# Layer 0 of a two-layer network: five attention stages of a slot queued one to two slots later

## The chip, the cores and the metric

The kernel runs on one core of a Trainium2 chip. The metric is device time in microseconds (us), the median over runs. A profile of one further execution shows what each engine did: TensorE (PE; PEld is its weight load), VectorE (DVE), ScalarE (ACT), GpSimd (POOL), and SyncE (SP), which here only issues DMAs.

## What is computed

The input is 8 images of 128x128 positions with 128 channels, in float32. Layer 0 is a linear attention with a normalization and a residual; layer 1 is a convolution, four selective scans and a gated normalization. The change touches layer 0 alone, whose reference is, cut to what matters:

```
qkv = einsum('bhwc,cf->bhwf', x, w_qkv)
q, k, v = split(qkv, 3)                     # each reshaped to (B, 4 heads, 32, N), N = H*W
q = softmax(q, axis=-2) * inv_scale         # over the 32 of a head
k = softmax(k, axis=-1)                     # over all positions
context = einsum('bhdn,bhen->bhde', k, v)
attn = einsum('bhde,bhdn->bhen', context, q)
out = einsum('bhwf,fc->bhwc', attn, w_out) + b_out
mu = mean(out); var = mean(square(out - mu))
out = (out - mu) * rsqrt(var + LN_EPS) * gamma + beta
return out + x
```

Layer 1 needs, beside this output, a gate z * sigmoid(z) of a projection of it; the kernel computes that gate within layer 0 too, by means of tanh.

## The kernel before

The program has three parts that run one after the other: `layer0`, `layer1_front` and `layer1_scan`. The profile is divided at about 2205 us, where the last gate of layer 0 is done.

In `layer0` an image of 128x128 positions is cut into 32 groups of 512 positions (`NG`), with the 128 channels on the partitions. Three kinds of work are staged over groups:

- **Context of an image** (`context(b)`): keys (`key`), a running maximum over blocks of four groups (`larger`, `fold`, `spread`), values (`value`), the difference to the maximum and its exponential (`subtract`, `raise_to`), and the sum of products k*v (`add`), which accumulates in PSUM and ends in a normalized 128x128 matrix.
- **Attention of an image** (`attend(b)`), which needs that matrix: `query` (PE pq; DVE qm, then q), `exponent` (ACT on q), `normalize` (DVE qs and its reciprocal, POOL's product with q), `through_wo` (PE pg, ACT copy gt), `through_context` (PE po, DVE o with the bias added, ACT square sq), `variance` (DVE var), `scale` (POOL: var, rstd by a power, and d, a diagonal of rstd), `turn` (PE pt, which scales and transposes), `finish` (ACT x1t, POOL's residual sum into x, and the store).
- **Gates of an image**: `ready` (a transposing copy v of a group, on POOL for the first gate of the coming slot and on ACT for the second, where the image's place asks for it), `gate_project` (two products pz on PE), `gate_tanh` (two on ACT), `gate_store` (two z on DVE, then two stores).

The order of the work is written out by hand. The loop of `image(b)` runs over slots `t`, and each slot calls every stage with the group that it treats: attention of image b for group t less a lag, and context of image b+1 for group a = t - `laters[b]`. The context manager `in_order` makes each engine keep exactly the order in which the stages were called. So an instruction that waits holds up everything behind it on its engine, and SP's stores keep that order as well.

Gates are planned beforehand (`plan`): while image b is attended, first the gates left over from image b-1 go out, two in a slot, then, once the attention of image b is through, its own gates, one in a slot. `laters[b]` is the number of slots needed for the left-over gates, plus two (`LEAD`), after which the context of the next image begins. The last image has no next context; its slots carry one left-over gate and, from slot 5 on, one of its own. So an image of the middle of the run consists of slots with attention and two gates, then slots with attention and a beginning context ("thin" slots), then slots with attention and context ("full"), and at the end slots with context and one own gate.

All small PSUM results of layer 0 (pq, pg, pz, pk, pv, po, pt and one of the maximum) share one pool of six buffers that go round: a new tile takes the buffer of the sixth before it, and waits until that has been read. SBUF buffers are q 3, gt 2, o 3, sq 2, d 2, z 4, v 4.

Of the kernel before, what the change touches and what calls it, by code (L numbers as in the profile page):

```python
# [26 lines left out]
NG = W // GW  # L27
# [50 lines left out]
def layer0(ctx: ExitStack, tc, xT, w_qkv, w_out, b_out, gamma, beta, win, x1, zs):  # L78
# [64 lines left out]
    def load(b, pieces=range(8)):  # L143
        for i in pieces:
            s = slice(16 * i, 16 * i + 16)
            nc.sync.dma_start(xs[b % 2][:, s, :], xT[ORDER[b], :, s, :])
# [3 lines left out]
    def ready(b, g, copy):  # L150

        v = group(b, g)
        if ORDER[b] % K < 2 or ORDER[b] < B // 2:
            t = wp.tile([P, GW, P], F32, name="v", bufs=4)
            copy(t, xs[b % 2].rearrange("p w h -> p h w")[:, g * GW : (g + 1) * GW, :])
            if ORDER[b] < B // 2:
                nc.sync.dma_start(x1[ORDER[b]][:, g * GN : g * GN + GN], t.rearrange("p w h -> p (w h)"))
            if ORDER[b] % K < 2:
                v = t
        vs[b, g] = v  # L160

    def gate_project(b, g):
        v = vs.pop((b, g))
        for c in range(NC2):
            pzs[b, g, c] = pz = ps.tile([P, GW, P], F32, name="pz", tag="ps")
            nc.tensor.matmul(pz, wz[:, c * P : c * P + P], v, start=True, stop=True)

    def gate_tanh(b, g, c):
        zts[b, g, c] = z = wp.tile([P, GW, P], F32, name="z", bufs=4)
        nc.scalar.activation(z, pzs[b, g, c], AF.Tanh)  # L170

    def gate_store(b, g, c):

        z = zts.pop((b, g, c))
        nc.vector.scalar_tensor_tensor(z, z, 1.0, pzs.pop((b, g, c)), ALU.add, ALU.mult)
        nc.sync.dma_start(zs[ORDER[b], c][:, g * GN : g * GN + GN], z.rearrange("p w h -> p (w h)"))
# [163 lines left out]
    for b in range(-1, B):  # L340
        left = NG - done[b - 1] if b > 0 else 0
        if b >= 0:
            laters[b] = -(-left // 2) + LEAD if left else 1
        for t in range(laters[b] + NG + BK + 2 if b < B - 1 else NG + 5):
            gates = plan[b, t] = []
            for _ in range(2 if b < B - 1 else 1):
                if b > 0 and done[b - 1] < NG:
                    gates.append((b - 1, done[b - 1]))
                    done[b - 1] += 1
                    if done[b - 1] == NG and b + 1 < B:  # L350
                        loads[b, t] = b + 1
            if b < B - 1:
                own = b >= 0 and not gates and t > NG + 2
            else:
                own = done[b] <= t - 5
            if own and done[b] < NG:
                gates.append((b, done[b]))
                done[b] += 1
# [4 lines left out]
    def image(b):  # L363

        key = larger = fold = spread = value = subtract = raise_to = add = None
        query = exponent = normalize = through_wo = through_context = None
        variance = scale = turn = finish = None
        if b + 1 < B:
            key, larger, fold, spread, value, subtract, raise_to, add = context(b + 1)
        if b >= 0:  # L370
            (query, exponent, normalize, through_wo, through_context, variance, scale, turn,
             finish) = attend(b)

        def at(stage, g):
            if stage is not None and 0 <= g < NG:
                stage(g)

        for t in (t for i, t in times if i == b):
            a = t - laters[b]
            first, second = (plan[b, t] + [None, None])[:2]  # L380
            at(scale, t - 2)
            at(finish, t - 3)
            at(query, t)
            at(through_wo, t - 1)
            for gates in plan[b, t]:
                gate_project(*gates)
            at(exponent, t)
            if first:
                for c in range(NC2):
                    gate_tanh(*first, c)  # L390
            at(subtract, a - BK - 1)
            at(raise_to, a - BK - 1)
            at(key, a)
            at(normalize, t)
            for gates, copy in zip(plan.get(then.get((b, t)), ()), (nc.gpsimd.tensor_copy, nc.scalar.copy)):
                ready(*gates, copy)
            if first:
                for c in range(NC2):
                    gate_store(*first, c)
            if second:  # L400
                for c in range(NC2):
                    gate_tanh(*second, c)
            at(fold, a - 1)
            at(value, a - BK - 1)
            at(larger, a)
            at(through_context, t - 1)
            if second:
                for c in range(NC2):
                    gate_store(*second, c)
            at(add, a - BK - 2)  # L410
            at(turn, t - 2)
            at(spread, a - 1)
            at(variance, t - 1)
            if (b, t) in loads:
                load(loads[b, t])

    with in_order(tc):
        load(0)
        load(1)
        for b in range(-1, B):  # L420
            image(b)
# [828 lines left out]
@with_exitstack  # L1250
def tile_kernel(ctx: ExitStack, tc, a, out):
    dram = ctx.enter_context(tc.tile_pool(name="dram", bufs=1, space=DRAM))
    x1 = dram.tile([B, P, L], F32, name="x1")
    ubs = dram.tile([B, 2, NC2, P, L], F32, name="ubs")
    xds = dram.tile([B, R + 2, L], F32, name="xds")
    xps = dram.tile([B, 2, 3, R + 2, L], BF16, name="xps")
    zs = dram.tile([B, NC2, P, L], F32, name="zs")
    gs = dram.tile([2, NC2, P, L], F32, name="gs")
    layer0(
        tc, a["x"], a["L0_conv_w_qkv"], a["L0_conv_w_out"], a["L0_conv_b_out"],  # L1260
        a["L0_conv_gamma"], a["L0_conv_beta"], a["L1_conv_Win"], x1, zs,
    )
    layer1_front(
        tc, x1, a["L1_conv_Win"], a["L1_conv_conv_w"], a["L1_conv_conv_b"], a["L1_conv_Wxproj"],
        a["L1_conv_D_param"], ubs, xds, xps, gs,
    )
    layer1_scan(
        tc, ubs, xps, zs, gs, a["L1_conv_dt_weight"], a["L1_conv_dt_bias"], a["L1_conv_A_log"],
        a["L1_conv_gamma"], a["L1_conv_beta"], a["L1_conv_Wout"], out,
    )  # L1270
# [40 lines left out]
```

## Time and profile before

| | us |
|---|---|
| median of 3 runs | 9080.09 (9077.24 to 9088.33) |
| profiled execution | 9087.79 |
| its span | 9086.0 |
| mean granted TensorE clock | 0.797 (1.00 in layer 0, 0.73 after it) |

| busy us | PE | PEld | DVE | ACT | POOL | DMA share |
|---|---|---|---|---|---|---|
| 0 to 2205 us (layer 0) | 2099.17 | 1283.15 | 1652.08 | 1370.79 | 1296.33 | 0.32 |
| 2205 to 9086 us (layer 1) | 4204.77 | 1805.48 | 6454.91 | 5663.61 | 6161.82 | 0.75 |

A row gives how long each engine was busy in that stretch. Matmuls are pipelined and their ends are modelled, so PE counts as busy for longer than its array is fed; the distance between the starts of successive matmuls is the better measure, and the one used below. Layer 0 is less than a quarter of the span, and layer 1 begins where it ends.

The largest waits within layer 0 (from 0 to 2080 us), with their sums and counts, are POOL's var for DVE's var (346.4 us, 237), ACT's sq for DVE's o (260.1 us, 195), POOL's q for DVE's qs (249.8 us, 21, one of them 115.9 us long before the first attention), ACT's exponential for DVE's q (170.2 us, 196) and DVE's var for ACT's sq (126.6 us, 176). PE waits 79.9 and 27.6 us for POOL's d, and 113.4 and 25.2 us for POOL's q (weight loads and matmuls).

### The profile page before, as it was taken

How to read it: one execution, taken by the hardware profiler on the slowest of the kernel's cores; microseconds unless marked ns; L12 is line 12 of the kernel's file. 1: busy time of each engine (PE TensorE's matmuls, PEld its weight loads, DVE VectorE, ACT ScalarE, POOL GpSimd, SP SyncE). 2: the span in 40 equal slices, each digit the busy share in tenths (PEclk: the TensorE clock that was granted, in tenths of full speed). 3: DMA queues.
4: the chain of work that ended last, by engine and by line, in shares of the span. 5: the costliest groups of instructions: out<-in, count | busy, mean ns of one | idle time of the engine just before them, and what ended most of it. 6: DMA issues, size and time to landing. Idle time of an engine off the chain costs nothing. (4 is left out here: it accounts for less than half of the span.)

```text
span 9086.0 us, 92120 instructions
## 1 busy us (share of the span) xinstructions
PE 6303.9 (69%) x24512; PEld 3088.6 (34%) x24512; DVE 8107.0 (89%) x8210; ACT 7034.4 (77%) x8046; POOL 7458.1 (82%) x4820
## 2 busy tenths in 40 slices
PE   8999999998999999997335436355373453634636
PEld 5556655564333333332003104022040230411403
DVE  6777777777999999998899999999999999999996
ACT  5666666665999999997788887888878788888785
POOL 3656766646789888887699998999989989999897
PEclk9999999999999999999557658566585575755757
DMA  1332323423687888889569578596785866858767
GB/s 77 140 119 110 130 98 149 164 94 135 217 245 255 249 242 243 244 243 258 157 176 258 168 213 235 167 259 179 206 244 159 242 197 193 255 153 231 217 177 209
DMA packets 934776, 1750.72 MB, mean 193 GB/s; under 512 B 150228, under 2 KB 376148, under 8 KB 926064
## 3 DMA queue, kind: packets, MB, share of 16 engines
q1 hardware_dynamic: 873328, 1509.92, 50.4%
q0 software_dynamic: 60928, 234.90, 14.0%
q8 instruction: 200, 3.28, 0.1%
q14 instruction: 320, 2.62, 0.1%
HBM read 1052.36 MB, written 692.12 MB: 192 GB/s over the span
## 5 line engine op out<-in xcount | busy, mean ns | idle before, releaser
L992 POOL TENSOR_TENSOR h<-ubt,sp 128x1024 f32<-128x1024 f32 x1024 | 2420.6, 2396 | 348.3 <-ACT mv L1099 112.4
L975 PE MATMUL px<-rows,dtw 128*128 128x512 bf16 x2048 | 953.5, 565 | 2263.8 <-DVE y L1042 1052.7
L575 DVE SCALAR_TENSOR_TENSOR acc<-xb,cw,acc 128x1024 f32<-128x1024 f32 x1024 | 1320.6, 1290 | 132.2 <-ACT xb L543 89.3
L567 POOL TENSOR_TENSOR tap<-tap 128x1024 f32<-128x1024 f32 x512 | 1223.1, 2392 | 248.8 <-ACT tap L565 224.9
L979 ACT ACTIVATE sp<-px 128x1024 f32<-128x1024 f32 x1024 | 1046.9, 1024 | 432.8 <-PE px L975 416.3
L975 PEld LDWEIGHTS <-dtw 128*128 128x128 bf16 x2048 | 169.0, 110 | 3087.5 <-issue 1022.8
L1002 DVE TENSOR_TENSOR_SCAN h<-px,h 128x1024 f32<-128x1024 f32 x512 | 1177.7, 2332 | 32.2 <-POOL h L992 29.1
L1000 DVE TENSOR_TENSOR_SCAN h<-px,h 128x1024 f32<-128x1024 f32 x512 | 1178.2, 2331 | 21.4 <-POOL h L992 18.7
L1050 POOL TENSOR_TENSOR y<-y,h 128x512 f32<-128x512 f32 x768 | 1162.8, 1561 | 3.9 <-DVE h L1023 3.9
L983 ACT ACTIVATE px<-sp,sa 128x1024 f32<-128x1024 f32 x1024 | 1110.4, 1109 | 6.1
L556 PE MATMUL acc<-xi,wt 128*128 128x512 f32 x2048 | 939.1, 601 | 54.1 <-ACT ures L580 54.1
L565 ACT ACTIVATE tap<-xb,cw 128x1024 f32<-128x1024 f32 x768 | 837.3, 1139 | 13.9 <-POOL xb L540 13.8
L979 ACT ACT_TABLE_LOAD x512 | 656.9, 1283 | 171.1 <-PE px L975 148.9
L983 ACT ACT_TABLE_LOAD x512 | 656.9, 1283 | 9.2
L1115 PEld LDWEIGHTS px<-wg,z 128*128 128x128 f32 x4096 | 582.8, 227 | 116.7 <-issue 110.8
L1115 PE MATMUL px<-wg,z 128*128 128x128 f32 x4096 | 581.9, 310 | 0.0
L1008 PE MATMUL pc<-rows,csel 128*128 128x512 bf16 x1024 | 517.6, 586 | 80.2 <-DVE rstd L1103 76.5
L556 PEld LDWEIGHTS acc<-xi,wt 128*128 128x128 f32 x2048 | 375.4, 190 | 575.5 <-issue 413.8
L286 POOL TENSOR_TENSOR q<-q,qs 128x512 f32<-128x512 f32 x256 | 270.3, 1056 | 313.8 <-DVE qs L285 249.8
L529 PE MATMUL pxb<-xi,wi 128*128 128x512 f32 x1024 | 498.2, 609 | 2.3 <-DMA xi<-x 1.2
L1042 DVE TENSOR_TENSOR y<-y,px 128x1024 f32<-128x1024 f32 x384 | 468.7, 1221 | 14.4
L1023 DVE TENSOR_TENSOR h<-h,pc 128x1024 f32<-128x1024 f32 x384 | 466.0, 1214 | 0.0
(154 smaller groups left out, 14923.0 us busy)
## 6 DMA issues: line engine op xcount, KB each, us to landing
ubt<-ubs SPq DMA_DIRECT2D x1024, 512.0 KB
zs<-z SPq DMA_DIRECT2D x512, 256.0 KB
ubs<-ures SPq DMA_DIRECT2D x256, 512.0 KB
ubs<-turned SPq DMA_DIRECT2D x256, 512.0 KB
z<-zs SPq DMA_DIRECT2D x256, 512.0 KB
y<-gs POOLq DMA_DIRECT2D x128, 1024.0 KB, 10.4
gs<-du POOLq DMA_DIRECT2D x96, 1024.0 KB, 8.7
rows<-xps SPq DMA_DIRECT2D x1536, 60.0 KB
```

Of the source, the lines that this page charges most:

```text
L556: nc.tensor.matmul(acc[:, s, :], wt[:, j, c, :], x, start=(j == 0), stop=(j == len(ON_PE) - 1))
L565: nc.scalar.activation(t, at(n, c, *d), AF.Copy, scale=weight(n, c, *d))
L567: nc.gpsimd.tensor_tensor(sums[n, c], sums[n, c], t, ALU.add)
L575: nc.vector.scalar_tensor_tensor(acc, at(n, c, *d), weight(n, c, *d), acc, ALU.mult, ALU.add)
L975: nc.tensor.matmul(p[:, hf * 512 : hf * 512 + 512], sl.dw[:, c * P : c * P + P], src, start=True, stop=True)
L979: nc.scalar.activation(t, da[n, c], AF.Softplus)
L983: nc.scalar.activation(da[n, c], sp[n, c], AF.Exp, scale=sa[:, sl.s, c : c + 1])
L992: nc.gpsimd.tensor_tensor(h, u, t, ALU.mult)
L1000: nc.vector.tensor_tensor_scan(e[:, ::-1], x[:, ::-1], e[:, ::-1], start, ALU.mult, ALU.add)
L1002: nc.vector.tensor_tensor_scan(e, x, e, start, ALU.mult, ALU.add)
L1050: nc.gpsimd.tensor_tensor(v[:, c], v[:, c], h[:, c], ALU.add)
L1115: nc.tensor.matmul(po[:, w, :], z[:, c, w * H : w * H + H], wg[:, c, :], start=(c == 0), stop=(c == NC2 - 1))
```

## The change

The stages themselves and their number stay the same. The lags and the order of their calls within a slot change:

- `normalize` treats group t-1 instead of t, and is called first in the slot.
- `through_context` treats t-2 instead of t-1, and is called ahead of the gates.
- `variance` treats t-3 instead of t-1, and is called ahead of `scale`.
- `scale` and `turn` treat t-3 instead of t-2, and `finish` t-4 instead of t-3.
- `through_wo` still treats t-1, but is called behind the gates' products, the first gate's tanh and the keys; `key` moves ahead of `raise_to`.
- The own gates of an image start one slot later, since the last group is finished one slot later. By the planner's rule the number of slots becomes 415 instead of 412, and `laters` changes from 16, 12, 11 and 11 to 17, 13, 12 and 12 for images 1, 3, 5 and 7.

```
-                own = b >= 0 and not gates and t > NG + 2
+                own = b >= 0 and not gates and t > NG + 3
...
-            at(scale, t - 2)
-            at(finish, t - 3)
+            at(normalize, t - 1)
+            at(variance, t - 3)
+            at(scale, t - 3)
+            at(finish, t - 4)
             at(query, t)
-            at(through_wo, t - 1)
+            at(exponent, t)
+            at(through_context, t - 2)
             for gates in plan[b, t]:
                 gate_project(*gates)
-            at(exponent, t)
             if first:
                 for c in range(NC2):
                     gate_tanh(*first, c)
             at(subtract, a - BK - 1)
+            at(key, a)
+            at(through_wo, t - 1)
             at(raise_to, a - BK - 1)
-            at(key, a)
-            at(normalize, t)
             for gates, copy in zip(plan.get(then.get((b, t)), ()), (nc.gpsimd.tensor_copy, nc.scalar.copy)):
                 ready(*gates, copy)
...
             at(fold, a - 1)
             at(value, a - BK - 1)
             at(larger, a)
-            at(through_context, t - 1)
             if second:
                 for c in range(NC2):
                     gate_store(*second, c)
             at(add, a - BK - 2)
-            at(turn, t - 2)
+            at(turn, t - 3)
             at(spread, a - 1)
-            at(variance, t - 1)
```

## Prediction

> **What bounds the kernel now.** I read the page first: its slices show where TensorE (PE) is full. Layer 0, all that the change touches, ends near 2205 us, so it is the first ten of 40 slices.
>
> ```profile
> PE   8999999998999999997335436355373453634636
> ```
>
> That reads as "PE-bound", but matmul busy time includes pipelining, so next I read PE's timeline at one full slot (attention and context work together, no gate).
>
> ```profile
> 1014.21 1.02 PE L272 MATMUL pq<-x,wq 128*128 128x512 f32 x2
> 1015.07 1.05 PE L292 MATMUL pg<-wo,q 128*128 128x128 f32 x8
> ...
> 1018.54 1.06 PE L244 MATMUL pc<-vt,k 128*128 128x129 f32 x8
> 1019.43 1.06 PE L325 MATMUL pt<-d,o 128*128 128x128 f32 x8
> 1020.32 1.02 PE L272 MATMUL pq<-x,wq 128*128 128x512 f32 x2
> ```
>
> Start to start, a product over 512 columns takes 0.86 us and a group of eight 0.89 us; the slot is 6.11 us with no gap. A gate pair is 4 passes, 1.72 us. So PE's work in a slot is: full 6.11; two gates 6.94 (0.86+0.89+3.44+0.86+0.89); one gate 5.22; attention alone 3.50, with the keys 4.36. Where is a slot longer? I took the starts of pq from the same view:
> - two gates: 6.94 in images 3 and 4, 7.0 to 7.8 in 1, 2, 5, 6. Nearly no loss.
> - full: 6.11. No loss.
> - the 9 thin slots between the last gate and the full ones: image 2 has 6.24, 5.05, 5.10, 5.05, 5.69, 5.64, 7.36, 5.22, 6.59 where PE's work is 3.50, 3.50, 4.36 (four times), 4.70, 5.22, 6.11.
> - image 7, one gate: 6.24 against 5.22.
>
> Starts less work, over layer 0, leave 163 us of PE stall: 11 before image 0, 18 in image 0, 107 in images 1 to 6, 28 in image 7. The 107 divide into 20 in two-gate phases, 73 in thin ones, 14 in the drains. What ends these waits is in VectorE's (DVE's) timeline, image 7:
>
> ```profile
> 2109.73 0.69 DVE L284 TENSOR_REDUCE qs<-q 128x16 f32<-128x512 f32 x1 [0.69 <-ACT q L279]
> 2110.45 0.25 DVE L285 RECIPROCAL qs<-qs 128x16 f32<-128x16 f32 x1
> 2110.62 1.22 DVE L175 SCALAR_TENSOR_TENSOR z<-z,pz 128x512 f32<-128x512 f32 x2
> 2111.75 0.68 DVE L300 TENSOR_TENSOR o<-po,bb 128x512 f32<-128x512 f32 x1
> 2113.19 0.69 DVE L306 TENSOR_REDUCE var<-sq 128x4 f32<-128x512 f32 x1 [0.76 <-ACT sq L302]
> 2113.80 0.68 DVE L274 TENSOR_REDUCE qm<-pq 128x16 f32<-128x512 f32 x1
> 2114.58 0.69 DVE L276 TENSOR_TENSOR q<-pq,qm 128x512 f32<-128x512 f32 x1
> 2115.97 0.69 DVE L284 TENSOR_REDUCE qs<-q 128x16 f32<-128x512 f32 x1 [0.69 <-ACT q L279]
> ```
>
> From qs to qs is 6.24 us, the slot itself. In-order queues close a ring: qs, reciprocal, two z, o, ScalarE's (ACT's) square, var, qm, q, ACT's exponential, qs. DVE leaves its queue's head to wait for ACT twice per slot. So the bound in thin and one-gate slots is this ring, not an engine. The same sum without the z is 5.1, with one more DVE operation 5.65: the thin slots' pitches. The method holds, and I use it on the new order.
>
> Two queues set the other limits. GpSimd (POOL) in a thin slot, and ACT in a two-gate slot:
>
> ```profile
> 699.29 1.04 POOL L286 TENSOR_TENSOR q<-q,qs 128x512 f32<-128x512 f32 x1
> 700.75 0.19 POOL L312 TENSOR_SCALAR var<-var 128x4 f32<-128x4 f32 x1 [0.41 <-DVE var L306]
> 701.02 1.02 POOL L314 TENSOR_TENSOR rstd<-var,half 128x4 f32<-128x4 f32 x1
> 702.12 1.04 POOL L317 TENSOR_TENSOR d<-ident,rstd 128x512 f32<-128x512 f32 x1
> 703.11 1.27 POOL L331 TENSOR_TENSOR x<-x1t,x 128x512 f32<-128x512 f32 x1
> 704.35 1.05 POOL L286 TENSOR_TENSOR q<-q,qs 128x512 f32<-128x512 f32 x1
> ```
>
> POOL's five instructions without their one wait (0.41) take 4.6 us: more than PE's 3.50 or 4.36.
>
> ```profile
> 659.20 0.63 ACT L279 ACTIVATE q<-q 128x512 f32<-128x512 f32 x1 [1.34 <-DVE q L276]
> 660.01 1.31 ACT L170 ACTIVATE z<-pz 128x512 f32<-128x512 f32 x2 [0.18 <-DMA zs<-z]
> 661.22 1.11 ACT L155 COPY v<-x 128x512 f32<-128x512 f32 x1
> 662.23 1.09 ACT L170 ACTIVATE z<-pz 128x512 f32<-128x512 f32 x2
> 663.19 0.64 ACT L302 ACTIVATE sq<-o 128x512 f32<-128x512 f32 x1
> ```
>
> The square stands last, behind both gates' tanh. This is what the change reverses.
>
> **What the Trainium skill says.** "Trainium Kernel Development and Optimization", Best Practices, advises against matmul busy time as a measure; the trace agrees (a one-gate slot looks 90% busy, 72.23 of 80 us in the table of stretches from 2110, with work of 5.22 in 6.24). "Perfetto Trace Analysis", DVE / Act Engine Instruction, puts the semaphore wait in a queue ahead of the engine and outside the profiled duration: hence starts, not durations, are added here. "ScalarE: Activation LUTs", What ACT_TABLE_LOAD costs, lets back-to-back activations overlap by about 93 ns; the trace shows 0.60 us tanhs 0.50 apart. "TensorE: Matmul & The Clock Gate", What's actually happening, gives half clock after an idle window; in image 7 the passes after a stall of 3 us take 0.85 instead of 0.43 us.
>
> **The change, part by part.** No instruction is added or removed. Each attention group runs one slot deeper, and the own gates of an image start one slot later, so 415 slots instead of 412; work per slot thins accordingly, and three more thin slots cost nothing that PE's work sum doesn't hold.
>
> *What goes.* The old ring is cut: exponential to qs and square to var now have most of a slot between them.
>
> *What comes, two-gate slots.* New DVE order: qs, reciprocal, var, qm, q, o, z a, z b, z c, z d. New ACT order: x1t, exponential, square, tanh a, b, gt, copy of v, tanh c, d. Behind the square, which waits for o, all four tanhs now stand; behind gt, which waits for PE's pg after the gate products, stand the copy and two tanhs. A new ring closes, from z c to the next z c, each step start to start in the two views above: z d 0.60, qs 0.60, reciprocal 0.73, var 0.17, qm 0.60, q 0.79, o 0.60, square 0.78, tanh a 0.52, tanh b 0.50, gt 0.50, copy 0.48, tanh c 0.97, z c 0.63: **8.45 us**, against 6.94 of PE. PE is drawn along, since a gate product takes the PSUM buffer that z c frees six tiles before. The old order's longest ring by the same sum is 6.5, below PE. POOL (4.6 and a copy of 1.0) fits. SP's queue too: copy's end to the next tanh over the z stores is 3.95 (663.55 to 667.50), with tanh b, gt and copy 6.6.
>
> Two-gate slots of images 1 to 6: 14, 6, 10, 8, 9, 9. Start: the first four slots are ramped; z c of slot 0 comes at 6.7 us as in image 3's trace (902.46 less 895.72), then 13.9, 21.8, 30.2, so the gate product of slot 4 starts at 31.0 where PE's work is 24.2: 6.8 lost. Each later slot loses 1.5; there are 26 of these. At the end pg waits for the last z d, qs, reciprocal and q's product: 3.1, and 0.8 more in five images with a single gate left. Sum 40.8+39.0+22.6 = 102, less the 20 stalled now: **+82**.
>
> *Thin slots.* Ring gone; now POOL's 4.6 binds, and DVE where it folds the maximum (two slots of about 5). The eight intervals after the first pg: 5.0+4x4.6+4.9+5.2+5.2 = 38.7 against work of 34.4, so 4.3 and 0.7 for the fold's wait: 5 an image, 30 instead of 73: **-43**.
>
> *Drains.* d is ready a slot ahead; the copy of v after the last group and the wait of pmx stay. About 1 of 2.3 an image: **-6**. *Image 0:* its first pg waits 3.6 instead of 4.5, and its seven thin slots go as above: **-7**.
>
> *Image 7.* No copies. Two gates: ring 7.5 (8.45-0.97) against 6.94 on 13 slots, +7. One gate: z a, z b 0.57, qs 0.56, reciprocal 0.72, var 0.17, qm 0.61, q 0.78, o 0.60, square 0.78, tanh 0.54, z 0.63 = 5.96 against 6.24 on 13 slots, -4. Start and tail lose about 2 less. **+1**, in which ±8 is open.
>
> *At nothing:* full slots (from 1010 to 1058 us DVE is busy 39.9, ACT 31.2, POOL 35.5 of 48; if that cover went, each 0.1 us costs 15 us over 150 slots), context-only slots with own gates, the next image's loads (landed well before the first keys: 11.6 us after issue now, some 9.4 then, while DMA moves 1 MB in about 2.5 us at the 420 GB/s of that stretch). Layer 1 runs the same code later or earlier; nothing hides layer 0.
>
> Sum: 82-43-6-7+1 = **+27 us** on the profiled 9087.8 (span 9086.0, 1.8 around it), so 9115. The median of the runs, 9080.1, is 7.7 less; carried over: **9107**.
>
> **Rivals.** *The new ring doesn't bind two-gate slots (faster).* Place: tanh behind square and gt. It decides at 6.94: if o and the square come early enough there, these phases lose 6 instead of 20 and image 7 gains 8 more: -14-43-6-7-7 = -77, **9003**. For it: from 640 to 676 us ACT is busy only 26.3 of 36. Against: low busy shares didn't prevent the 6.24 ring. Chance 0.14. *The ring binds, but half as hard* (7.7 us, by earlier starts): 30 us less, no change, **9077**. Chance 0.20. *Full slots lose too (slower still):* gt and the value copy, now late in PE's order, hold ACT 0.35 us a slot: +52, **9159**. Against: 1.5 us of room. Chance 0.10. That the order isn't what it says can't be: each engine keeps the order written.
>
> **How the numbers follow.** Main case 0.56, alone 9085 to 9130. A difference under 0.2% (18 us) can't be told from no change. Slower: 0.50 of the main case, 0.05 of the second rival and the third, 0.65; faster: the first and 0.04 of the second, 0.18; same: the rest, 0.17. Range 9045 to 9150, where thin slots gain 20 more and lose 20 less.
>
> **What would show it.** Right: two-gate slots of images 1 to 6 at 8.4 to 8.5, image 7's at 7.5 and 6.0, thin slots at 4.6 to 5, ACT's z waiting behind sq and gt, no wait of var for sq. Wrong: two-gate slots at 6.94, or full slots above 6.2.

## The result, and the profile after

| | before | after |
|---|---|---|
| median of 5 runs, us | 9083.94 (9077.24 to 9088.33) | 9121.03 (9115.49 to 9126.21) |
| ratio to before | | 1.0042, interval 1.0031 to 1.0053 |
| profiled execution, us | 9087.79 | 9121.03 |
| last gate product of layer 0 ends at | 2204.9 | 2249.1 |

The change makes the kernel slower by 37 us, where +27 was forecast. (With the runs made beside the experiments below, the median of before settles at 9080.6, the figure that differences further down start from.) All of it is in layer 0, which ends 44.2 us later in the profiles. Layer 1 takes 6870 us after and 6881 before; in the profiles of the experiments below, which all run the same layer 1, it takes 6869 to 6877, so that difference is scatter between executions.

The slice row of the page, which was the first line shown before, says almost nothing of this; layer 0 still reads as full:

```profile
PE   8999999998999999998335436345363453643636
```

VectorE's (DVE's) timeline after the change, in a two-gate slot of image 2 (columns: start, duration, instruction, and in brackets the idle time before it with what ended it), shows where the slot's length comes from:

```profile
671.45 1.28 DVE L175 SCALAR_TENSOR_TENSOR z<-z,pz 128x512 f32<-128x512 f32 x2 [1.16 <-ACT z L170]
672.65 0.68 DVE L284 TENSOR_REDUCE qs<-q 128x16 f32<-128x512 f32 x1
673.37 0.25 DVE L285 RECIPROCAL qs<-qs 128x16 f32<-128x16 f32 x1
673.53 0.63 DVE L306 TENSOR_REDUCE var<-sq 128x4 f32<-128x512 f32 x1
674.08 0.68 DVE L274 TENSOR_REDUCE qm<-pq 128x16 f32<-128x512 f32 x1
674.86 0.69 DVE L276 TENSOR_TENSOR q<-pq,qm 128x512 f32<-128x512 f32 x1
675.47 0.68 DVE L300 TENSOR_TENSOR o<-po,bb 128x512 f32<-128x512 f32 x1
677.39 1.28 DVE L175 SCALAR_TENSOR_TENSOR z<-z,pz 128x512 f32<-128x512 f32 x2 [1.24 <-ACT z L170]
679.84 1.28 DVE L175 SCALAR_TENSOR_TENSOR z<-z,pz 128x512 f32<-128x512 f32 x2 [1.16 <-ACT z L170]
```

And ScalarE's (ACT's) timeline of the same slot:

```profile
675.59 0.63 ACT L279 ACTIVATE q<-q 128x512 f32<-128x512 f32 x1 [3.01 <-DVE q L276]
676.24 0.63 ACT L302 ACTIVATE sq<-o 128x512 f32<-128x512 f32 x1
676.78 1.07 ACT L170 ACTIVATE z<-pz 128x512 f32<-128x512 f32 x2
677.73 0.59 ACT L294 COPY gt<-pg 128x512 f32<-128x512 f32 x1
678.20 1.11 ACT L155 COPY v<-x 128x512 f32<-128x512 f32 x1
679.18 1.11 ACT L170 ACTIVATE z<-pz 128x512 f32<-128x512 f32 x2
```

From one z c (671.45) to the next (679.84) it is 8.39 us, and the starts can be walked round: on DVE z d, qs, reciprocal, var, qm, q and o take 4.02 us to the start of o (675.47); then over to ACT, square 0.77, two tanhs from 0.54 later on, gt, copy of v and tanh c at 679.18, 3.71 us in all; then 0.66 back to z c. DVE idles 1.24 and 1.16 us and ACT 3.01 us in the slot, each waiting for the other. No engine is full. That is the ring of the forecast, which had 8.45.

TensorE's (PE's) starts of pq, slot by slot, confirm it: 8.36 to 8.40 us in the two-gate slots of images 1 to 6 once the first five are over, 7.40 in image 7 (forecast 7.5), 5.94 with one gate (5.96), 6.11 in the full slots as before.

Counted as before, starts less work, PE's stalls in layer 0 are (here slot by slot, which puts their sum 2 us above the forecast's 163):

| us of stall | before | after | after, forecast |
|---|---|---|---|
| gate slots, images 1 to 6 | 19.9 | 92.5 | 102 |
| thin slots | 73.6 | 56.9 | 30 |
| full slots | 1.1 | 0.6 | as before |
| drains | 13.7 | 8.5 | 8 |
| image 0 | 17.9 | 14.1 | 11 |
| image 7 | 28.3 | 28.9 | 29 |
| before image 0 | 10.7 | 7.8 | 11 |
| sum | 165.2 | 209.3 | 191 |

The sum grows by 44.1, as layer 0 does. One row is well off the forecast: the thin slots. Their pitches in image 2, after the last gate, are 5.94, 4.61, 4.61, 4.62, 5.94, 5.33, 6.64, 5.22: the 4.61 is POOL's, as forecast, but the three slots after it, in which DVE takes the running maximum of the keys, are longer. DVE's timeline after, in the first of them:

```profile
713.55 0.69 DVE L194 TENSOR_TENSOR run<-pk,k 128x512 f32<-128x512 f32 x1 [1.23 <-ACT k L186]
714.16 0.68 DVE L284 TENSOR_REDUCE qs<-q 128x16 f32<-128x512 f32 x1
...
716.97 0.68 DVE L300 TENSOR_TENSOR o<-po,bb 128x512 f32<-128x512 f32 x1
718.88 0.69 DVE L196 TENSOR_TENSOR run<-pk,run 128x512 f32<-128x512 f32 x1 [1.23 <-ACT k L186]
```

and ACT's beside it:

```profile
717.09 0.63 ACT L279 ACTIVATE q<-q 128x512 f32<-128x512 f32 x1 [2.25 <-DVE q L276]
717.75 0.63 ACT L302 ACTIVATE sq<-o 128x512 f32<-128x512 f32 x1
718.28 0.57 ACT L186 COPY k<-pk 128x512 f32<-128x512 f32 x1
```

The running maximum reads the keys that ACT copies, and ACT's copy now stands behind the exponential and the square, both of which wait for DVE. That is another ring of the same kind: maximum, qs, reciprocal, var, qm, q, o, square, key copy, maximum: 718.88 - 713.55 = 5.33 us, one of the pitches above, and 5.33 again to the next maximum at 724.21. The forecast left it out.

The table of waits after, over 0 to 2245 us (us in total, times, longest), has the whole trade in six lines:

```profile
ACT q L279 <- DVE q L276: 563.7, 256, 4.3
DVE z L175 <- ACT z L170: 277.8, 343, 5.6
DVE run L196 <- ACT k L186: 88.7, 128, 2.5
ACT sq L302 <- DVE o L300: 15.0, 17, 1.5
POOL var L312 <- DVE var L306: 10.9, 14, 1.5
ACT gt L294 <- PE pg L292: 1.3, 3, 0.8
```

The list shown before stopped at 2080 us; over the whole of layer 0 before (0 to 2205 us) sq for o was 291.1, POOL's var for DVE's var 379.7 and gt for pg 101.4: those waits did go. In their place ACT's exponential waits 563.7 instead of 185.9, z for tanh 277.8 instead of 119.1, and the maximum for the key copy 88.7 instead of 43.5.

### The profile page after: what moved, and what is told of

It reads as the page before. It is cut to its first block, busy times and chain, and to the rows that moved or that the text cites. A ratio compares the mean times of both kernels' runs of the same rounds, so it can differ in the third digit from the quotient of the medians.

```text
span 9119.2 us, 91835 instructions
## 1 busy us (share of the span) xinstructions
PE 6241.5 (68%) x24350; PEld 3085.5 (34%) x24512; DVE 8108.9 (89%) x8210; ACT 7023.7 (77%) x8046; POOL 7455.4 (82%) x4820
## 5 line engine op out<-in xcount | busy, mean ns | idle before, releaser
L975 PE MATMUL px<-rows,dtw 128*128 128x512 bf16 x1893 | 910.1, 573 | 2304.2 <-DVE y L1042 1060.7
L1000 DVE TENSOR_TENSOR_SCAN h<-px,h 128x1024 f32<-128x1024 f32 x512 | 1177.8, 2330 | 21.2 <-POOL h L992 18.8
L279 ACT ACTIVATE q<-q 128x512 f32<-128x512 f32 x256 | 161.3, 630 | 563.7 <-DVE q L276 563.7
L175 DVE SCALAR_TENSOR_TENSOR z<-z,pz 128x512 f32<-128x512 f32 x512 | 337.0, 685 | 282.1 <-ACT z L170 282.1
```

Source lines behind the costliest of these rows:

```text
L975: nc.tensor.matmul(p[:, hf * 512 : hf * 512 + 512], sl.dw[:, c * P : c * P + P], src, start=True, stop=True)
L1000: nc.vector.tensor_tensor_scan(e[:, ::-1], x[:, ::-1], e[:, ::-1], start, ALU.mult, ALU.add)
```

## The experiments

The theory: three rings of in-order queues set the slots, namely the two-gate ring (square and copy ahead of tanhs), the one-gate ring and the ring of the thin slots in which the maximum is taken ("keyed" below). The rivals: the tanhs are held by gt and its wait for pg; or the order of PE's own products and its six PSUM buffers set the slot; or ACT's load as such is what counts; later on, the DMA rate or the order of the stores.

In the table, "end" is the end of the last gate product of layer 0. A ratio is to the kernel before on the same chip; below, "after" is the changed kernel, which each run but the last starts from.

| kernel | time, us | ratio (interval) | end | two gates, image 3 | image 7, two gates | one gate |
|---|---|---|---|---|---|---|
| before | 9083.94 | | 2204.9 | 6.94 | 6.94 | 6.24 |
| after | 9121.03 | 1.0042 (1.0031 to 1.0053) | 2249.1 | 8.39 | 7.40 | 5.94 |
| 1, square later | 9066.54 | 0.9984 (0.9977 to 0.9991) | 2191.0 | 7.75 | 6.94, 7.27 | 5.28 |
| 2, second tanh earlier | 9060.89 | 0.9977 (0.9969 to 0.9986) | 2190.1 | 7.13 | 6.94 to 7.39 | 5.94 |
| 3, product with wo earlier | 9248.65 | 1.0185 (1.0168 to 1.0202) | 2378.8 | 8.45 | 8.08 | 6.43 |
| 4, keys earlier | 9114.32 | 1.0035 (1.0022 to 1.0048) | 2238.3 | 8.39 | 7.40 | 5.94 |
| 5, two copies in the ring | 9171.36 | 1.0098 (1.0084 to 1.0111) | 2297.1 | 9.07 | 8.08 | 5.94 |
| 6, two copies outside it | 9120.44 | 1.0043 (1.0029 to 1.0056) | 2245.1 | 8.33 | 7.34 | 5.94 |
| 7, moves of 1, 2 and 4 | 9045.71 | 0.9959 (0.9945 to 0.9973) | 2174.2 | 6.94 | 6.94 | 5.28 |
| 8, and the gates' stores first | 9006.00 | 0.9918 (0.9904 to 0.9931) | 2136.1 | 6.94 | 6.94 | 5.28 |
| 9, before with its stores first | 9064.72 | 0.9984 (0.9977 to 0.9990) | 2189.2 | 6.94 | 6.94 | 6.24 |

**1. The square behind the second gate's tanhs.** The square becomes a stage of its own.

```
             nc.vector.tensor_tensor(o, po, bb, ALU.add)
+
+        def square(g):
             vs[g] = sq = wp.tile([P, GW, P], F32, name="sq")
-            nc.scalar.activation(sq, o, AF.Square)
+            nc.scalar.activation(sq, os[g], AF.Square)
...
                     gate_tanh(*second, c)
+            at(square, t - 2)
             at(fold, a - 1)
```

> The changed kernel with one move: the square of o is issued behind both gates' tanh instead of ahead of the first. Ring theory (DVE's z c, z d, qs, reciprocal, var, qm, q, then ACT up to tanh c and back to z c): o and its square drop out, the exponential takes their place (0.72 instead of 0.60+0.78 us, tanh a 0.53 behind it), so two-gate slots of images 1 to 6 fall from 8.39 to 7.8 us, those of image 7 from 7.40 to PE's 6.94, its one-gate slots from 5.94 to 5.3; thin slots with keys, where the key copy no longer stands behind the square, from 5.3 to 4.7. In all about 50 us less than the changed kernel, near 9070. Rival theory (the order of PE's own products and the six PSUM buffers is what costs): nothing on PE moves, so slots stay at 8.39 and the time at 9121.

The pitches came as the ring says, and the kernel is 54 us faster than after and faster than before: gate stalls fall from 92.5 to 65.1, thin ones from 56.9 to 42.3, image 7's from 28.9 to 14.8. ACT's timeline in image 3 shows the order and what is left of the ring, now entered by the exponential:

```profile
925.67 0.63 ACT L279 ACTIVATE q<-q 128x512 f32<-128x512 f32 x1 [2.50 <-DVE q L276]
926.21 1.06 ACT L170 ACTIVATE z<-pz 128x512 f32<-128x512 f32 x2
...
929.59 0.65 ACT L304 ACTIVATE sq<-o 128x512 f32<-128x512 f32 x1
...
933.40 0.63 ACT L279 ACTIVATE q<-q 128x512 f32<-128x512 f32 x1 [2.50 <-DVE q L276]
```

The tanhs start 0.54 us behind the exponential instead of 1.19, and o and the square are out of the ring: 7.73 us from exponential to exponential. In the keyed slots 5.29, 4.67, 6.54 replace 5.94, 5.33, 6.64; 4.7 was expected for the 5.33. Nothing was moved on PE, so the rival of PE's own order is out.

**2. The second gate's tanhs behind the first's.** Ahead of gt and the copy, that is.

```
                     gate_tanh(*first, c)
+            if second:
+                for c in range(NC2):
+                    gate_tanh(*second, c)
...
-            if second:
-                for c in range(NC2):
-                    gate_tanh(*second, c)
```

> The changed kernel with one move: the second gate's two tanh are issued right behind the first gate's, ahead of gt and the copy of v. Ring theory: gt (0.50) and the copy (0.97) leave the ring, 8.39 becomes 7.0, next to PE's 6.94; image 7's two-gate slots 7.40 become 6.94; its one-gate slots stay at 5.94 and thin slots stay as they are. About 65 to 75 us less than the changed kernel, near 9050. Rival theory (PE's order and buffers): no change, 9121.

With gt and the copy out of the ring 7.13 us is left in images 3 and 4. The thin slots don't change (55.7 us of stall), as they shouldn't: they have no gates. But in images 1, 2, 5 and 6 the slots vary between 6.94 and 9.0 us, and the time is 11 us above the 9050 expected. These four images are those in whose gate slots copies of v are stored; that is taken up in 7 and 8.

**3. The product with wo ahead of the gates.** Here gt stands ahead of the tanhs and no longer waits behind the gates' products.

```
             at(through_context, t - 2)
+            at(through_wo, t - 1)
...
-            at(through_wo, t - 1)
             at(raise_to, a - BK - 1)
```

> The changed kernel with one move: the product through w_out and its copy gt are issued ahead of the gates, behind the product with the context. Ring theory: gt stays between the square and tanh c, it only changes places with tanh a and b, so two-gate slots stay at 8.4 and the time within 10 us of 9121. Rival theory (tanh c and d are late because gt before them waits for pg, which PE now has behind the gate products): gt no longer waits, two-gate slots fall to about 7.5 and the time by some 45 us.

Against the rival: two-gate slots stay at 8.45 and don't fall to 7.5, so it is not gt's wait for pg that lengthens them; nor has gt such a wait after the change (1.3 us in all, in the table above). The time, however, missed by far: 128 us above after. The first slots of an image take 8 to 13 us instead of 7 to 10, image 7's two-gate slots 8.08, its one-gate slots 6.43, and every fourth full slot 7.48 instead of 6.45. The waits of layer 0 in 3:

```profile
PE pg L292 <- POOL q L286: 194.7, 153, 4.8
ACT gt L294 <- PE pg L292: 12.1, 13, 1.4
```

Read from the trace, without a run of its own: on PE, pg now stands ahead of the gates' products and waits there for POOL's product (24.3 us in 27 waits after). So pg, the gates' products, tanh d, z d, qs, reciprocal, POOL's product and pg close a ring through PE's queue; in image 7 it takes 8.07 us from pg (2189.63) to pg (2197.70). gt's own wait is small, but gt now stands ahead of the tanhs and of the key copy, and so in the one-gate ring and the keyed ring as well: both are longer by 0.49 (6.43 for 5.94, 5.82 for 5.33). I had moved a stage out of one place and lengthened or made three rings. The full slots were not followed up.

**4. The keys ahead of the exponential.**

```
             at(query, t)
+            at(key, a)
             at(exponent, t)
...
-            at(key, a)
```

> The changed kernel with one move: the keys' product and their copy are issued ahead of the exponential, so ACT copies the keys before it waits for q and o. Theory for the thin slots (the running maximum on DVE waits for ACT's copy of the keys, which the change leaves behind the square, and that closes a ring q, o, square, key copy, maximum, qs, reciprocal, var, qm, q of 5.3 us): the third to fifth slots with keys, now 5.94, 5.33 and 6.64, fall to about 4.6, 4.7 and 5.2, some 3 us an image, 15 to 20 us in all, near 9104; two-gate slots stay at 8.39. Rival (GpSimd's 4.6 us and the block's maximum make these slots long): no change.

The keyed slots become 4.95, 4.62 and 6.27, and the thin stalls fall from 56.9 to 40.3; the wait of the maximum for the key copy falls from 88.7 to 24.3 us. So that ring is shown. But only 7 us of time came of it (10.8 in the profiles' layer 0): drains rose from 8.5 to 13.1, and the third slot stays at 6.27 instead of the 5.2 expected. DVE's timeline in it:

```profile
719.65 0.68 DVE L196 TENSOR_TENSOR run<-pk,run 128x512 f32<-128x512 f32 x1
720.37 1.07 DVE L201 TENSOR_REDUCE top<-run 128x128 f32<-128x512 f32 x1
721.35 0.68 DVE L284 TENSOR_REDUCE qs<-q 128x16 f32<-128x512 f32 x1
```

The fold's reduction, 0.98 us from start to start, stands ahead of qs, and with qs POOL's whole chain to d is later; PE then waits 1.11 us for d. This reading of the fold slot was not tried by itself.

**5 and 6. Padding inside and outside the ring.** Two copies of a spare tile, which nothing reads, in every two-gate slot: in 5 ahead of the second gate's tanhs, in 6 behind them. ACT's load is the same in both.

```
             if second:
+                nc.scalar.copy(spare, spare)
+                nc.scalar.copy(spare, spare)
```

> The changed kernel with two spare copies of 128x256 on ScalarE (about 0.29 us each, by the 0.50 us step of a 128x512 copy) in each two-gate slot, between the copy of v and the second gate's tanh, that is inside the ring. Ring theory: two-gate slots go from 8.39 to about 8.97 us, image 7's from 7.40 to 7.98; some 40 and 14 slots, 30 us in all, near 9151. Rival (ScalarE has room, 0.7 busy, and PE's order sets the slot): unchanged, 9121.

> The same two copies in the same slots, but behind the second gate's tanh, where ScalarE next waits for DVE's q: outside the ring. Ring theory: two-gate slots stay at 8.39 and 7.40, the time within 5 us of 9121. Rival (ScalarE's total work per slot is what counts): the same 30 us as inside the ring.

ACT's timeline of 5 in image 3:

```profile
955.42 1.11 ACT L157 COPY v<-x 128x512 f32<-128x512 f32 x1
956.41 0.43 ACT L405 COPY spare<-spare 128x256 f32<-128x256 f32 x1
956.87 0.40 ACT L406 COPY spare<-spare 128x256 f32<-128x256 f32 x1
957.18 1.08 ACT L172 ACTIVATE z<-pz 128x512 f32<-128x512 f32 x2
```

The copies put 0.77 us between the copy of v and tanh c, and the slot grows by 0.68, in images 1 to 6 and in image 7 alike: 50 us. Behind the tanhs the same copies cost nothing (9120.44 against 9121.03; the slot is 8.33). So it isn't ACT's load that matters here, but its place in the ring. I had expected +30 for 5: a pair was taken as 0.58, and the first slots of an image, not counted, lengthened as well (8.08 and 10.64 for the third and fourth, after: 7.34 and 9.89). In the Trainium skill, "Perfetto Trace Analysis", Optimization Strategy, says that consistent bubbles can mean too little SBUF or PSUM for the next tile. Here no buffer was added in 1 or 2 and the gap shrank (8.39 to 7.75 and 7.13 in image 3), so in this case the order sufficed; whether more buffers would have helped too was not tried.

**7. The moves of 1, 2 and 4 together.**

> The three moves that helped, together: square behind all tanh, second tanh behind the first, keys ahead of the exponential. Ring theory: the longest ring in a two-gate slot is 6.4 us, below PE's 6.94; one-gate slots 5.3, keyed thin slots 4.6 to 5. Only in images 1, 2, 5 and 6, where v is also stored, the chain copy of v, SyncE, z store, next tanh (3.95 us and the tanhs, gt and copy) can hold a slot at 7 to 8. About 90 to 100 us less than the changed kernel, 9021 to 9031, and so below the kernel before by 50 to 60. Rival: the gains don't add, because GpSimd and the start of each image bind next: near 9050.

Images 3, 4 and 7 are at PE's work: 6.94 with two gates, and one-gate slots have 5.28 against 5.22. But 9045.71 is outside the theory's 9021 to 9031 and beside the rival's 9050. What is missing is in images 1, 2, 5 and 6 again: 7.42 us with a 9.3 to 10.7 every few slots; 48.4 of the 53.9 us of gate stall are there. The queue of SP (which issues the DMAs) over 0 to 2200 us says what it waits for in 7:

```profile
SPq L157 <- POOL v L155: 739.2, 39, 279.4
...
SPq L176 <- DVE z L175: 411.9, 287, 4.8
SPq L157 <- ACT v L155: 112.1, 38, 4.8
```

L157 stores the copy of v, L176 the z. (Most of the 739.2 us are stretches in which no store is due, one of them 279.4 long; the counts and the last line matter.) The store of a v that ACT hasn't copied yet stands ahead of z that are done (112.1 us in 38 waits, up to 4.8 each), and the tanhs need z's buffers back. The table of waits of 7 has that too:

```profile
ACT z L170 <- DMA zs<-z: 18.4, 16, 2.1
```

ACT's timeline of 7, in image 2, shows the pitch of 7.42 us from one copy of v to the next:

```profile
654.27 1.09 ACT L155 COPY v<-x 128x512 f32<-128x512 f32 x1
...
658.21 2.60 ACT L170 ACTIVATE z<-pz 128x512 f32<-128x512 f32 x4 [0.62 <-PE pz L166]
...
661.69 1.08 ACT L155 COPY v<-x 128x512 f32<-128x512 f32 x1
```

From the copy over SP's stores to the first tanh it is 3.94 us, and 3.48 over the tanhs, the square and gt to the next copy. (The tanh's wait is put down to pz, whose product had been done for over a microsecond; that it was for z's buffer is an inference.)

**8. The gates' stores first.** Run 7 with both gates' stores called ahead of the copies of v and their stores. Not a byte more or less is moved, and in the two traces the order of instructions in layer 0 differs on SP alone. Against 7:

```
-            for gates, copy in zip(plan.get(then.get((b, t)), ()), (nc.gpsimd.tensor_copy, nc.scalar.copy)):
-                ready(*gates, copy)
...
-            at(fold, a - 1)
-            at(value, a - BK - 1)
-            at(larger, a)
             if second:
                 for c in range(NC2):
                     gate_store(*second, c)
+            for gates, copy in zip(plan.get(then.get((b, t)), ()), (nc.gpsimd.tensor_copy, nc.scalar.copy)):
+                ready(*gates, copy)
+            at(fold, a - 1)
+            at(value, a - BK - 1)
+            at(larger, a)
```

> As the run with three moves, and both gates' z and their stores are issued ahead of the copies of v and their stores, so that on SyncE a z store never waits for a copy. Theory (SyncE's order lengthens two-gate slots of images 1, 2, 5, 6): these slots at 6.94 to 7.1, 10 to 15 us less than the run with three moves. Rival (the bandwidth of the stores does it): no difference.

SP's waits in 8:

```profile
SPq L157 <- POOL v L155: 672.8, 7, 280.8
SPq L176 <- DVE z L175: 546.7, 419, 4.4
...
SPq L157 <- ACT v L155: 4.9, 15, 0.4
```

The stores of v wait seldom and the stores of z in their place, which is harmless; no tanh waits for a store of z any more. PE's timeline in image 2:

```profile
643.09 1.02 PE L272 MATMUL pq<-x,wq 128*128 128x512 f32 x2
643.96 1.02 PE L298 MATMUL po<-gt,ctxn 128*128 128x512 f32 x2
644.81 3.60 PE L166 MATMUL pz<-v,wz 128*128 128x512 f32 x8
648.25 1.05 PE L292 MATMUL pg<-wo,q 128*128 128x128 f32 x8
649.14 1.06 PE L327 MATMUL pt<-d,o 128*128 128x128 f32 x8
650.03 1.02 PE L272 MATMUL pq<-x,wq 128*128 128x512 f32 x2
```

6.94 us without a gap, and so in every image from the fifth slot on. Gate stalls are 16.3 us, 2.7 or 2.8 in each image. Expected were 10 to 15 us less than 7; it is 40 less. The rival, that these images were held by the DMA rate, falls, since the same bytes went out faster. This kernel beats both: 75 us less than before.

**9. The kernel before with its stores first.** Is 8 merely the order of the stores? One move in the kernel before. Here it changes ACT's queue as well: the copy of v, which stood between the two gates' tanhs, now stands behind all four and the square.

```
             at(normalize, t)
-            for gates, copy in zip(plan.get(then.get((b, t)), ()), (nc.gpsimd.tensor_copy, nc.scalar.copy)):
-                ready(*gates, copy)
...
                     gate_store(*second, c)
+            for gates, copy in zip(plan.get(then.get((b, t)), ()), (nc.gpsimd.tensor_copy, nc.scalar.copy)):
+                ready(*gates, copy)
             at(add, a - BK - 2)
```

> The kernel before with one move: the copies of v and their stores are called behind the second gate's stores, so that SP's stores of v stand behind the stores of z. Nothing of the staging of the attention is changed. Theory (order of the stores is a small matter of its own, what the best kernel gains comes from the deeper staging with its ring opened): the two-gate slots of images 1, 2, 5 and 6, 7.0 to 7.8 us before, become 6.94; of the 20 us of stall in gate slots about 6 stay at the turns, so 8 to 14 us less; thin slots (6.24, 5.05, 5.10 ...) and image 7's 6.24 stay; time about 9068. Rival (most of the best kernel's 75 us is the order of the stores, which would help the kernel before as much as it helped the three moves): 30 us or more less, below 9050.

As the theory had it: 15 us, two-gate slots at 6.94 from each image's third on, gate stalls 9.7 instead of 19.9, and tanh's 18.8 us of waiting for stores of z gone; thin slots still lose 68.9 and one-gate slots stay at 6.24. So of the 75 us that 8 gains, this move gives 15 without the deeper staging; how much of the 15 is SP's order and how much ACT's was not separated. The other 60 come with the deeper staging once its rings are opened; whether other orders of the kernel before could reach as far was not tried.

## Why the prediction was right, and where it was off

- *The new two-gate ring binds, at 8.45* (its steps as printed add up to 8.47). Right: 8.39, and 7.40 for 7.5 in image 7. Opened by taking members out (1 and 2), lengthened by putting one in (5), untouched by the same load outside (6). gt's wait for pg, which the forecast named beside the square, is not a cause: it comes to 1.3 us in all, and with gt ahead of the tanhs (3) the slot is the same. Its 102 us came as 92.5. The first rival (the ring doesn't bind, 9003) and the second (7.7 us, 9077) are ruled out by the pitch itself.
- *One-gate slots, 5.96.* Right (5.94). Image 7's balance came as +0.6 for +1.
- *Full slots lose nothing.* Right: 6.11. The third rival (9159) is out.
- *Drains -6, image 0 -7.* -5.2 and -3.8; before image 0, 2.9 less where nothing was forecast.
- *Thin slots -43.* Here a term of the sum was mis-sized: the stall left was put at 30 us and is 56.9, so the gain was 17. POOL's 4.6 was right for the slots before the first maximum. The term took "ring gone" for the keyed slots too, though the change leaves the key copy behind the exponential and the square: the maximum's wait for it, a line in the table of waits before (43.5 us), was not carried into the new order. Run 4 shows the wait's part, 16.6 us of thin stall. The slot with the fold's reduction was put at 5.2 and is 6.64, and 6.27 without that wait; that rest is read from the trace only.
- *The total.* The thin slots lose 27 us more than forecast, the gates 9.5 less, and the other rows nearly cancel: 44 instead of 27 in layer 0. The sum came nearer than its worst term because a smaller error the other way met it, not because that term was right. (Part of both errors is only where a wait is counted: the last gate slot's wait runs over into the first thin one; taken together the two rows grew by 55.9, forecast 39, which leaves the same 17.) The median came 14 us above the forecast.

What stays open: why the drains lengthen by 4.6 us in 4, what lengthens every fourth full slot in 3, and the 0.09 us by which the slot grows less than the padding in 5.

## What to carry to other kernels

Before reordering stages on in-order queues, list every wait of one engine for another in the new order and walk each ring that two queues close, start to start; here a slot was as long as the longest ring or the fullest engine, and the busy shares did not show the rings. After staging something deeper, queue what waits for fresh data behind whatever doesn't need it: the same deeper staging cost 37 us with the square, the tanhs and the key copy in the wrong order, and with them and the stores in the right one the kernel was 75 us faster than before, 15 of which the moved copies and stores gave without it. To prove a ring, pad it: the same dummy work inside (+50 us) and outside (nothing).

## What had not been expected

- SP's queue, kept in order, was a ring member like an engine: stores moved past each other, with no byte changed and no other engine's order touched, were worth 40 us once the other rings were open (7 to 8). In the kernel before, with ACT's copy moved too, it was 15 us.
- The gains don't add, in either direction: 1, 2 and 4 alone took 54, 60 and 7 us off after, together 75 where the three add up to 121, and with the order of the stores 115.
- In 5 a 128x256 copy lasting 0.40 to 0.43 us added only 0.34 us to the slot (0.68 for two), while the distance between its neighbours grew by 0.385.
